# Eight gated blocks on one core: where remainders, preparations and the 32-largest search are placed

## The chip, the core and the metric

The kernel runs on one core of a Trainium2 chip. The metric is the device time of one execution in microseconds (us), lower is better. Engines: PE (TensorE, the matmuls), VectorE (DVE), ScalarE (ACT), GpSimd (POOL), and the queue SP, which issues the DMAs. Each engine executes its own instructions in the order in which the program holds them, and waits on semaphores for the others.

## The reference

Eight sequences of 256 tokens with 128 features pass through four pairs of blocks. Each block reads the layer norm of x and adds its result to x, scaled by a tanh gate:

```
x = x + tanh(g_xattn[0]) * L0_xattn(layernorm(x), ctx)   # causal linear attention, 16 heads
x = x + tanh(g_ffn[0])   * L0_ffn(layernorm(x))          # self attention, 16 heads, plus 8 experts (top 2)
x = x + tanh(g_xattn[1]) * L1_xattn(layernorm(x), ctx)   # 8 heads of 64, only the 64 largest scores of a row
x = x + tanh(g_ffn[1])   * L1_ffn(layernorm(x))          # 8 experts (top 2) and a shared one
x = x + tanh(g_xattn[2]) * L2_xattn(layernorm(x), ctx)   # attention, 16 heads of 8
x = x + tanh(g_ffn[2])   * L2_ffn(layernorm(x))          # 8 wide experts (top 2) and a shared one
x = x + tanh(g_xattn[3]) * L3_xattn(layernorm(x), ctx)   # 16 heads of 8, only the 32 largest scores of a row
x = x + tanh(g_ffn[3])   * L3_ffn(layernorm(x))          # 16 experts in the q, k, v and output projections of one head
```

## The kernel before, in words

The eight sequences form four groups of two (g = 0 to 3); a group is 512 tokens, four tiles of 128. x stays on the chip (xs[g]). For one group a block is a stage, named x0, f0, f1, x2, f2 and f3 in the code (cross attention and feed-forward part of blocks 0 to 3). The attentions of blocks 1 and 3 are no such stages: they choose the 64 or 32 largest scores of a row, a long job for VectorE, and run as one second stream beside all others.

So two streams of Python generators write the program. `others` goes through the stages in a fixed list: x0(0), x0(1), f0(0), x0(2), f0(1), x0(3), f0(2), f1(0), f0(3), x2(0), f1(1), f2(0), x2(1), f1(2), f2(1), x2(2), f1(3), f2(2), x2(3), f2(3), f3(0) to f3(3). Each stage has a share: 40 for x0, 53 for f0, 35 for f1, 75 for x2, 80 for f2, 95 for f3, which makes 1512 in all, and f3(0) begins at 1132. `largest_scores` runs the 64-largest stage (block 1) and then the 32-largest stage (block 3). `side_by_side` always lets that stream emit that stands at the lower position. `T_START` gives the second stream its positions on the same scale: the start of the 64-largest stage, its end, the start of the 32-largest stage, the position at three quarters of it, and its end. A stream that may not go on yet yields None, and the other one goes ahead.

A tile scheduler then orders the recorded instructions; what stands in an engine's queue follows these positions closely, but not to the letter.

Three gates tie the streams together. A group enters the 64-largest stage when its f0 is settled (`started`), f1(g) waits for that stage (`largest_1`). A group enters the 32-largest stage when its f2 is settled (`middle`). f3(0) waits until groups 0 and 2 have left that stage (`largest_3`).

The search stages work in 32 chunks each: eight batches (one sequence each) of four chunks. For the 32-largest stage a chunk is four heads, 8 rows of scores for each partition. The steps of one chunk k:

- `fetch(k)`: scores on PE (line 420), copied to a room in SBUF by ScalarE (427).
- `largest`: four rounds of MAX8 (385) and MATCH_REPLACE8 (389) on VectorE for each of the 8 rows, 32 MAX8 in all; the mask on GpSimd (392). Half way, `fetch(k + 1)` is emitted.
- `weigh(k - 1)`, beside the search of the next chunk: the row's maximum is taken from the scores by `shifted` (for block 3 two transposes on PE, line 1382, and an addition to qT on VectorE, line 1383), then the scores once more on PE (574), the mask added by matmuls (584), the exponential eK on ScalarE (599), and the products with v. After the fourth chunk of a batch, `finish` transposes back, divides (`heads_back`, 341 to 348) and projects out (`out_proj`, 319 to 333), once for each of the two tiles, and adds to x (`add_gated`, 290).

Helpers spread such work. `Ahead(steps, gen)` takes steps of a generator as the neighbouring body goes on: `up_to(f)` at share f of the body. In `others` the end of a stage (its remainder: the last out projections, the addition to x) is taken during the first 30% of the next body, after which the stage counts as settled; the next stage's preparation (layer norm, router, first q, k, v) is taken from 30% to 90%:

```
behind.up_to(f / 0.3)
if f > 0.3:
    settle()
    ...
        ahead.up_to((f - 0.3) / 0.6)
```

In the search stage `weigh` is such a remainder too, with 4 steps, or 12 after the last chunk of a batch.

Other lines named below: the scores of x2 and f0 for their maxima (687, reduced on VectorE at 695) and for the weights (723); f2's matmuls (1476 and 1445, Gelu at 1477); f1's (1269); f3's (1580, 1581 with w3a; 1582, 1635 with w3b; the scaled inputs xe at 851). f2 loads two 256 KB weights an expert, f3 loads w3a and w3b once, all on SP.

Of the kernel before, what the change touches and what calls it, by code (L numbers as in the profile page):

```python
# [14 lines left out]
ALU = mybir.AluOpType  # L15
AX = mybir.AxisListType

P = 128
D = 128
B = 8  # L20
S = 256
# [69 lines left out]
def gated_blocks_kernel(ctx: ExitStack, tc: tile.TileContext, a, out):  # L91
# [9 lines left out]
    def program(exact):  # L101
# [8 lines left out]
        def bank(name="bank"):  # L110
            return psum.tile([P, 512], F32, tag="bank", name=name, bufs=4)
# [8 lines left out]
        def out2(name):  # L120
            return act.tile([P, 512], F32, tag="out2", name=name, bufs=6)
# [165 lines left out]

        def add_gated(g, t, src, gate):

            nc.vector.scalar_tensor_tensor(xs[g][:, t, :], src, gate, xs[g][:, t, :], ALU.mult, ALU.add)  # L290

        def heads_T(w, src, bias, scale, tag):

# [23 lines left out]
            nc.scalar.copy(va[:, :, :, 0:8], pp.rearrange("p t (h d) -> p t h d", d=8))  # L317
            return va

        def out_proj(g, t, o_sb, chunks, w, bias, gate):  # L320

            pt = bank("pt_o")
            for c in range(chunks):
                nc.tensor.transpose(pt[:, c * P : (c + 1) * P], o_sb[:, c * P : (c + 1) * P], ident)
            oT = out2("oT")
            nc.scalar.copy(oT[:, 0 : chunks * P], pt[:, 0 : chunks * P])
            yield
            po = bank("po")
            for c in range(chunks):
                nc.tensor.matmul(  # L330
                    po[:, 0:D], lhsT=oT[:, c * P : (c + 1) * P], rhs=w[:, c, :], start=(c == 0), stop=False
                )
            nc.tensor.matmul(po[:, 0:D], lhsT=bias, rhs=biases, start=False, stop=True)
            add_gated(g, t, po[:, 0:D], gate)

        def heads_back(g, bb, oTs, done):

            for qc in range(2):
                pn = bank("pn").rearrange("p (c r d) -> p c r d", c=4, r=4)
                for c in range(4):  # L340
                    nc.tensor.transpose(
                        pn[:, c].rearrange("p r d -> p (r d)"), oTs[c // 2][:, c % 2, qc * P : (qc + 1) * P], ident
                    )
                rec = small.tile([P, 4, 4], F32, tag="rec", name="rec")
                nc.vector.reciprocal(rec, pn[:, :, :, 8])
                o_sb = out2("o_sb")[:, 0:D].rearrange("p (c r d) -> p c r d", c=4, r=4)
                nc.vector.tensor_tensor(
                    o_sb, pn[:, :, :, 0:8], rec.unsqueeze(3).to_broadcast([P, 4, 4, 8]), ALU.mult
                )
                yield  # L350
                yield from done(g, 2 * bb + qc, o_sb.rearrange("p c r d -> p (c r d)"))

        def chunk_products(o, va, c, es):

# [41 lines left out]
        def attention_largest(  # L396
# [9 lines left out]
            NP = R // 2  # L406
            NJ = 2 * R
            batches = [(g, bb) for g in groups for bb in range(2)]
            ready, ahead, masks, shifts, placed = {}, {}, {}, {}, {}
            n = len(batches) * 4  # L410

            def fetch(k):
# [117 lines left out]
            def keep_largest(k):  # L530
# [25 lines left out]
                for j in range(NJ):  # L556
# [3 lines left out]
                        accum_out=dropped[:, NJ * k + j : NJ * k + j + 1],  # L560
                    )

            def weigh(k):

                i, c = divmod(k, 4)
                qT, kT, va = ready[i]
                mask = masks.pop(k)
                row = shifted(shifts.pop(k), qT, c)
                yield
                sps = [pair("sw").rearrange("p (r n q) -> p r n q", r=2, n=2) for _ in range(NP)]  # L570
                for m in range(2):
                    for r in range(R):
                        rs = slice(rows * r, rows * r + rows)
                        nc.tensor.matmul(  # L574
                            sps[r // 2][:, r % 2, m, :], lhsT=kT[rs, c, m * P : (m + 1) * P], rhs=qT[rs, c, :],
                            start=(m == 0), stop=False,
                        )
                for r in range(R):
                    for m in range(2):
                        sp = sps[r // 2][:, r % 2, m, :]  # L580
                        if row is not None:
                            nc.tensor.matmul(sp, lhsT=pick[:, r : r + 1].to_broadcast([P, P]), rhs=row, start=False, stop=False)
                        for qc in range(2):
                            nc.tensor.matmul(  # L584
                                sp[:, qc * P : (qc + 1) * P], lhsT=mask[:, r, qc, m * P : (m + 1) * P], rhs=drop,
                                start=False, stop=(m == 1 and qc == 1),
                            )
                if dropped is not None and not search:

                    for h in range(NP):  # L590
                        kept = act.tile([P, NJ // NP, S], BF16, tag="s", name="kept", bufs=2)
                        nc.scalar.activation(  # L592
                            kept, mask[:, 2 * h : 2 * h + 2].rearrange("p r q k -> p (r q) k"), AF.Copy,
                            accum_out=dropped[:, NP * k + h : NP * k + h + 1],
                        )
                es = []
                for sp in sps:
                    e = work("eK").rearrange("p (r n q) -> p r n q", r=2, n=2)
                    nc.scalar.activation(e, sp, AF.Exp)  # L599
# [52 lines left out]
            for k in range(steps):  # L652
                for f in units(k):
                    if f is not None:
                        behind.up_to(f)
                        look_ahead(k, f)
                    yield None if f is None else (k + f) / steps
                behind.finish()

                done = k - 1  # L660
                if 0 <= done < n:
                    behind = Ahead(4 if done % 4 < 3 else 12, weigh(done))
            for _ in alongside((x / 12 for x in range(1, 13)), behind):
                yield 1.0

# [412 lines left out]

        class block0_ffn:
            def __init__(self, g):  # L1080
                def done(g, t, o):
                    add_gated(g, t, o, tgf[:, 0:1])
                    yield

                self.g, self.att = g, attention_T(g, self.operands, done)
# [256 lines left out]
        def context_operands(n, weights, k=""):  # L1342
            wq, wk, wv, wo, bq, bk, bo = weights
            norms = {}

            def prepare(g, bb):
                if g not in norms:
                    norms[g] = yield from layer_norm(g)
                xnT = norms[g][1][:, bb * S : (bb + 1) * S]
                cT = ctxT[:, g * W + bb * S : g * W + (bb + 1) * S]  # L1350
                kT = heads_T(wk, cT, bk, 1.0, "kT" + k)
                yield
                qT = heads_T(wq, xnT, bq, INV_SQRT8, "qT" + k)
                yield
                return qT, kT, values16(wv, cT, 32, "va" + k)

            def done(g, t, o):
                yield from out_proj(g, t, o, 1, wo.unsqueeze(1), bo, tgx[:, n : n + 1])
                yield

            return prepare, done
# [353 lines left out]

        T_START = (140, 595, 600, 1140, 1330)

        def stages():  # L1720

# [77 lines left out]
        def others():  # L1799
# [12 lines left out]
            for i, (g, share, may, prep, steps, body, after) in enumerate(todo):  # L1812
                if ahead is None:
                    settle()
                    while not may():
                        yield None
                    ahead = Ahead(steps, prep())
                while ahead.step():
                    yield t
                operands, ahead = ahead.value, None  # L1820
                gen = body(operands)
                following = todo[i + 1] if i + 1 < len(todo) and todo[i + 1][0] != g else None
                while True:
                    try:
                        f = next(gen)
                    except StopIteration as end:
                        settle()
                        behind, done = end.value, after
                        break
                    behind.up_to(f / 0.3)  # L1830
                    if f > 0.3:
                        settle()
                        if following and following[2]():
                            if ahead is None:
                                ahead = Ahead(following[4], following[3]())
                            ahead.up_to((f - 0.3) / 0.6)
                    yield t + share * f
                t += share
            settle()
# [48 lines left out]
```

## Time and profile before

| | before |
|---|---|
| device time, median of 3 runs | 2550.43 us (2545.41 to 2565.9) |
| profiled execution | 2546.42 us, span 2544.7 us |
| mean granted TensorE clock | 0.862 |
| PE busy | 2123.7 us (83%), 12068 records |
| VectorE busy | 1762.5 us (69%) |
| ScalarE busy | 1149.0 us (45%) |
| GpSimd busy | 879.8 us (35%) |
| DMA | 32.97 MB, 13 GB/s over the span |
| the 32-largest stage, first to last MAX8 of line 385 | 1192.5 to 2347.4 us |
| first f3 matmul (line 1580) | 2135 us |

Busy is the share of the span in which an engine has an instruction in work; a PE that is busy need not be at its peak, since matmuls are pipelined and slow down with the granted clock. A fp32 matmul of the program leaves two records. The 40 digits of a slice row stand for 63.6 us each, in tenths.

### The profile page before, as it was taken

How to read it: one execution, taken by the hardware profiler on the slowest of the kernel's cores; microseconds unless marked ns; L12 is line 12 of the kernel's file. 1: busy time of each engine (PE TensorE's matmuls, PEld its weight loads, DVE VectorE, ACT ScalarE, POOL GpSimd, SP SyncE). 2: the span in 40 equal slices, each digit the busy share in tenths (PEclk: the TensorE clock that was granted, in tenths of full speed). 3: DMA queues.
4: the chain of work that ended last, by engine and by line, in shares of the span. 5: the costliest groups of instructions: out<-in, count | busy, mean ns of one | idle time of the engine just before them, and what ended most of it. 6: DMA issues, size and time to landing. Idle time of an engine off the chain costs nothing.

```text
span 2544.7 us, 35734 instructions
## 1 busy us (share of the span) xinstructions
PE 2123.7 (83%) x12068; PEld 1292.4 (51%) x12094; DVE 1762.5 (69%) x5463; ACT 1149.0 (45%) x2437; POOL 879.8 (35%) x2252
## 2 busy tenths in 40 slices
PE   7998888887878778888989868899676975988898
PEld 5655455554445444445444435445343444666677
DVE  4635757756765667665899879894798869798332
ACT  2236556546554677864355433464333542322101
POOL 3104434434432464531334324341233334233000
PEclk8999889978988889998599966899775986999999
DMA  2000001000000000010001100021000110000000
GB/s 63 6 1 2 1 1 32 1 1 1 1 1 1 1 26 1 26 34 22 1 1 42 34 1 1 1 59 50 1 1 1 42 42 1 1 5 1 5 5 6
DMA packets 47896, 32.97 MB, mean 13 GB/s; under 512 B 4747, under 2 KB 42838, under 8 KB 47702
## 3 DMA queue, kind: packets, MB, share of 16 engines
q1 hardware_dynamic: 47702, 30.58, 4.2%
q8 instruction: 97, 1.59, 0.3%
q14 instruction: 97, 0.79, 0.1%
HBM read 29.53 MB, written 1.05 MB: 12 GB/s over the span
## 4 chain that ended last, share of the span: by engine, by line
DVE 39%; PE 36%; ACT 13%; POOL 8%; issue 4%; DMA 0%; DVEq 0%; SPq 0%; ACTq 0%; POOLq 0%
DVE m L385 13%; DVE wk L389 12%; ACT signs L495 4%; PE sm L687 3%; PE sw L723 3%; PE ph L1476 3%; PE pp L299 3%; PE y L1445 2%; DVE nmz L695 2%; PE po L1635 2%; ACT sign L495 2%; PE oT L357 2%; PE o L1216 2%; DVE xe L851 2%; DVE list L542 1%
## 5 line engine op out<-in xcount | busy, mean ns | idle before, releaser
L392 POOL TENSOR_SCALAR mask<-rooms,m 128x256 bf16<-128x256 f32 x192 | 223.3, 1163 | 385.5 <-DVE m L385 353.4
L385 DVE MAX8 m<-wk 128x8 f32<-128x256 f32 x768 | 326.8, 426 | 37.0 <-DVE wk L389 0.9
L723 PE MATMUL sw<-qT,kT 32*128 32x256 f32 x1024 | 172.4, 476 | 68.3 <-ACT eK L599 24.1
L695 DVE TENSOR_REDUCE nmz<-sm 128x4 f32<-128x1024 f32 x128 | 154.9, 1219 | 105.1 <-PE sm L687 96.6
L389 DVE MATCH_REPLACE8 wk<-m,wk 128x256 f32<-128x256 f32 x512 | 208.9, 408 | 0.0
L495 ACT ACTIVATE signs<-room,nt 128x256 bf16<-128x256 f32 x288 | 145.9, 507 | 128.7 <-POOL nt L527 78.5
L687 PE MATMUL sm<-kT,qT 32*128 32x256 f32 x1024 | 152.6, 440 | 40.0 <-DVE nmz L695 28.4
L592 ACT ACTIVATE kept<-mask 128x1024 bf16<-128x1024 bf16 x64 | 67.6, 1057 | 227.3 <-POOL mask L392 227.1
L1476 PE MATMUL ph<-xnT,we 128*128 128x512 f32 x288 | 156.2, 638 | 15.5 <-ACT hT L1477 7.4
L723 PEld LDWEIGHTS sw<-qT,kT 32*128 32x128 f32 x1024 | 101.0, 222 | 128.4 <-DVE nmz L695 32.3
L737 ACT ACTIVATE eT<-sw 128x1024 f32<-128x1024 f32 x128 | 129.6, 1019 | 79.9 <-PE sw L723 73.9
L574 PE MATMUL sw<-qTk,kTk 32*128 32x256 f32 (+1 forms) x768 | 120.8, 456 | 53.6 <-DVE qTk L1383 35.2
L1445 PE MATMUL y<-hT,we 128*128 128x512 f32 x288 | 146.0, 620 | 0.6 <-DVE wb_sb L1457 0.6
L687 PEld LDWEIGHTS sm<-kT,qT 32*128 32x128 f32 x1024 | 92.3, 205 | 101.0 <-DVE nmz L695 42.9
L1477 ACT ACTIVATE hT<-ph,b 128x512 f32<-128x512 f32 x144 | 98.4, 686 | 98.8 <-PE ph L1476 94.4
L599 ACT ACTIVATE eK<-sw 128x1024 f32<-128x1024 f32 x96 | 96.6, 1019 | 89.4 <-PE sw L584 88.5
L420 PE MATMUL sp<-kTk,qTk 32*128 32x256 f32 (+1 forms) x768 | 121.1, 448 | 14.8 <-ACT eT L737 6.5
L357 PE MATMUL oT<-eT,va 128*32 128x256 f32 x1024 | 120.6, 449 | 10.2 <-ACT eT L737 9.3
L392 POOL TENSOR_SCALAR mask<-room,m 128x256 bf16<-128x256 f32 x64 | 74.5, 1164 | 155.2 <-DVE m L385 152.8
L574 PEld LDWEIGHTS sw<-qTk,kTk 32*128 32x128 f32 (+1 forms) x768 | 71.5, 212 | 96.1 <-issue 42.4
L420 PEld LDWEIGHTS sp<-kTk,qTk 32*128 32x128 f32 (+1 forms) x768 | 72.5, 209 | 59.5 <-issue 17.0
L387 POOL TENSOR_SCALAR nmk<-m 128x1 f32<-128x1 f32 x256 | 59.5, 232 | 100.7 <-DVE m L385 100.6
(381 smaller groups left out, 4976.2 us busy)
## 6 DMA issues: line engine op xcount, KB each, us to landing
we<-in_L_ffn_exp_w_dram SPq DMA_DIRECT2D x64, 256.0 KB
we<-in_L_ffn_shared_w_dram SPq DMA_DIRECT2D x8, 256.0 KB
x<-in_x_dram SPq DMA_DIRECT2D x4, 256.0 KB
big_ctx<-in_ctx_dram SPq DMA_DIRECT2D x4, 256.0 KB
w1f<-in_L_ffn_fc_w_dram SPq DMA_DIRECT2D x1, 1024.0 KB
w3a<-in_L_ffn_q_proj_dram SPq DMA_DIRECT2D x4, 256.0 KB
w3a<-in_L_ffn_k_proj_dram SPq DMA_DIRECT2D x4, 256.0 KB
w3b<-in_L_ffn_v_proj_dram SPq DMA_DIRECT2D x4, 256.0 KB
```

What stands on the lines that cost most here:

```text
L357: nc.tensor.matmul(o[32 * r : 32 * r + 32, :], lhsT=va[:, n, 4 * c + r, :], rhs=es[r // 2][:, r % 2, n, :], start=(n == 0), stop=(n == 1),)
L385: nc.vector.max(m8, src[:, j, :])
L389: nc.vector.match_replace(wk[:, j, :], m8, src[:, j, :], LOWEST)
L392: nc.gpsimd.tensor_scalar(mask[:, j, :], s[:, j, :], m8[:, 7:8], 1.0, ALU.is_lt, ALU.mult)
L420: nc.tensor.matmul(sps[r // 2][:, r % 2, qc, :], lhsT=qT[rs, c, qc * P : (qc + 1) * P], rhs=kT[rs, c, :], start=(qc == 0), stop=(qc == 1),)
L495: nc.scalar.activation(to, s[:, j, :], AF.Sign, bias=nt[:, j : j + 1], accum_out=acc[:, j : j + 1])
L574: nc.tensor.matmul(sps[r // 2][:, r % 2, m, :], lhsT=kT[rs, c, m * P : (m + 1) * P], rhs=qT[rs, c, :], start=(m == 0), stop=False,)
L687: nc.tensor.matmul(sps[r // 2][:, r % 2, j, :], lhsT=qT[rs, 2 * cp + j, qc * P : (qc + 1) * P], rhs=kT[rs, 2 * cp + j, :], start=(j == 0), ...
L695: nc.vector.tensor_reduce(nmz[:, qc, 2 * cp : 2 * cp + 2, 2 * h : 2 * h + 2, 8].rearrange("p c r -> p r c"), sps[h], AX.X, ALU.max, negate ...
L723: nc.tensor.matmul(sps[r // 2][:, r % 2, n, :], lhsT=kT[rs, c, n * P : (n + 1) * P], rhs=qT[rs, c, :], start=(n == 0), stop=(n == 1),)
L1445: nc.tensor.matmul(y, lhsT=w2[:, c, :], rhs=hs[c // 2][:, js], start=(c == 0), stop=(c == 3))
L1476: nc.tensor.matmul(pp[:, js], lhsT=w1[:, c * P : (c + 1) * P], rhs=xnT, start=True, stop=True)
```

## The change

The positions of the search stages move: (140, 595, 600, 1140, 1330) becomes (150, 595, 610, 1170, 1380). Remainders of a stage are taken over 40% of the next body in place of 30%, preparations from 40% to 90% in place of 30% to 90%. `weigh` has 3 and 11 steps in place of 4 and 12, and the shift by the maxima is taken out of it: `shift_scores` emits it for chunk k - 1 beyond 0.6 of step k, where `weigh` emitted it at the start of step k + 1. `heads_back` collects both tiles of a batch in one o_sb and calls `done` once, one yield later; `out_proj` and `add_gated` then treat both tiles together. The two projections still take a pair of matmuls each.

```diff
         def add_gated(g, t, src, gate):
 
-            nc.vector.scalar_tensor_tensor(xs[g][:, t, :], src, gate, xs[g][:, t, :], ALU.mult, ALU.add)
+            x = xs[g][:, 2 * t : 2 * t + 2, :] if len(src.shape) == 3 else xs[g][:, t, :]
+            nc.vector.scalar_tensor_tensor(x, src, gate, x, ALU.mult, ALU.add)
...
-        def out_proj(g, t, o_sb, chunks, w, bias, gate):
+        def out_proj(g, bb, o_sb, w, gate, bias):
 
             pt = bank("pt_o")
-            for c in range(chunks):
-                nc.tensor.transpose(pt[:, c * P : (c + 1) * P], o_sb[:, c * P : (c + 1) * P], ident)
-            oT = out2("oT")
-            nc.scalar.copy(oT[:, 0 : chunks * P], pt[:, 0 : chunks * P])
+            for qc in range(2):
+                nc.tensor.transpose(pt[:, qc * P : (qc + 1) * P], o_sb[:, qc * P : (qc + 1) * P], ident)
+            oT = out2("oT")[:, 0:S]
+            nc.scalar.copy(oT, pt[:, 0:S])
             yield
-            po = bank("po")
-            for c in range(chunks):
-                nc.tensor.matmul(
-                    po[:, 0:D], lhsT=oT[:, c * P : (c + 1) * P], rhs=w[:, c, :], start=(c == 0), stop=False
-                )
-            nc.tensor.matmul(po[:, 0:D], lhsT=bias, rhs=biases, start=False, stop=True)
-            add_gated(g, t, po[:, 0:D], gate)
+            po = bank("po")[:, 0:S].rearrange("p (t d) -> p t d", t=2)
+            for qc in range(2):
+                nc.tensor.matmul(po[:, qc, :], lhsT=oT[:, qc * P : (qc + 1) * P], rhs=w, start=True, stop=False)
+                nc.tensor.matmul(po[:, qc, :], lhsT=bias, rhs=biases, start=False, stop=True)
+            add_gated(g, bb, po, gate)
 
         def heads_back(g, bb, oTs, done):
 
+            o_sb = out2("o_sb")[:, 0:S]
             for qc in range(2):
...
-                o_sb = out2("o_sb")[:, 0:D].rearrange("p (c r d) -> p c r d", c=4, r=4)
                 nc.vector.tensor_tensor(
-                    o_sb, pn[:, :, :, 0:8], rec.unsqueeze(3).to_broadcast([P, 4, 4, 8]), ALU.mult
+                    o_sb[:, qc * P : (qc + 1) * P].rearrange("p (c r d) -> p c r d", c=4, r=4), pn[:, :, :, 0:8],
+                    rec.unsqueeze(3).to_broadcast([P, 4, 4, 8]), ALU.mult,
                 )
                 yield
-                yield from done(g, 2 * bb + qc, o_sb.rearrange("p c r d -> p (c r d)"))
+            yield
+            yield from done(g, bb, o_sb)
...
+            def shift_scores(k):
+
+                if 0 <= k < n:
+                    i, c = divmod(k, 4)
+                    rows_of[k] = shifted(shifts[k], ready[i][0], c)
+
             def weigh(k):
...
-                row = shifted(shifts.pop(k), qT, c)
-                yield
+                shifts.pop(k)
+                row = rows_of.pop(k)
...
                     if f is not None:
+                        if f > 0.6 and k - 1 not in rows_of:
+                            shift_scores(k - 1)
                         behind.up_to(f)
                         look_ahead(k, f)
                     yield None if f is None else (k + f) / steps
+                if k - 1 not in rows_of:
+                    shift_scores(k - 1)
                 behind.finish()
 
                 done = k - 1
                 if 0 <= done < n:
-                    behind = Ahead(4 if done % 4 < 3 else 12, weigh(done))
+                    behind = Ahead(3 if done % 4 < 3 else 11, weigh(done))
...
-        T_START = (140, 595, 600, 1140, 1330)
+        T_START = (150, 595, 610, 1170, 1380)
...
-                    behind.up_to(f / 0.3)
-                    if f > 0.3:
+                    behind.up_to(f / 0.4)
+                    if f > 0.4:
                         settle()
...
-                            ahead.up_to((f - 0.3) / 0.6)
+                            ahead.up_to((f - 0.4) / 0.5)
```

The callers follow: block 0's `done` hands both tiles to `add_gated`, block 2's and 3's hand them to `out_proj` in one call.

More of the change, by code (lines that the diff above doesn't have):

```diff
@@ L408, in attention_largest @@
             batches = [(g, bb) for g in groups for bb in range(2)]
-            ready, ahead, masks, shifts, placed = {}, {}, {}, {}, {}
+            ready, ahead, masks, shifts, placed, rows_of = {}, {}, {}, {}, {}, {}
             n = len(batches) * 4
@@ L1080, in __init__, with done @@
             def __init__(self, g):
-                def done(g, t, o):
-                    add_gated(g, t, o, tgf[:, 0:1])
+                def done(g, bb, o):
+                    add_gated(g, bb, o.rearrange("p (t d) -> p t d", t=2), tgf[:, 0:1])
                     yield
@@ L1355, in prepare, with done @@
                 return qT, kT, values16(wv, cT, 32, "va" + k)
-            def done(g, t, o):
-                yield from out_proj(g, t, o, 1, wo.unsqueeze(1), bo, tgx[:, n : n + 1])
+            def done(g, bb, o):
+                yield from out_proj(g, bb, o, wo, tgx[:, n : n + 1], bo)
                 yield
```

## The prediction

> **What bounds the kernel now.** I read the page first (busy shares by slice and the chain that ended last), then the times of line 385's MAX8 instructions (32 to a chunk of the 32-largest stage), then the windows between these times, then PE's waits.
>
> ```profile
> PE   7998888887878778888989868899676975988898
> DVE  4635757756765667665899879894798869798332
> PEclk8999889978988889998599966899775986999999
> DVE m L385 13%; DVE wk L389 12%; ACT signs L495 4%; PE sm L687 3%; PE sw L723 3%; PE ph L1476 3%; PE pp L299 3%; PE y L1445 2%; DVE nmz L695 2%; PE po L1635 2%; ACT sign L495 2%; PE oT L357 2%; PE o L1216 2%; DVE xe L851 2%; DVE list L542 1%
> ```
>
> Two engines take turns. PE is at 8 to 9 tenths nearly everywhere except in a few slices from the 24th on, where VectorE stands at 9; a quarter of the chain is the 32-largest search (lines 385 and 389). The windows cut the program at the search's own marks: before it, chunks 0-7, 8-15, 16-23, 24-31, and the rest after its last MAX8.
>
> ```profile
> 190.00:1192.00 1002.00, 837.92 (x5126) 490.34 (x5135) 651.57 (x1916) 602.85 (x1537) 424.43 (x1518) 0.88 0.03 10
> 1192.50:1482.30 289.80, 255.69 (x1223) 132.13 (x1227) 246.80 (x813) 137.60 (x207) 105.07 (x157) 0.85 0.06 17
> 1482.30:1797.50 315.20, 271.11 (x1350) 144.96 (x1350) 249.86 (x811) 141.63 (x213) 107.55 (x158) 0.82 0.08 23
> 1797.50:2071.10 273.60, 201.20 (x966) 106.26 (x964) 222.27 (x769) 109.48 (x180) 105.19 (x152) 0.74 0.07 20
> 2071.10:2347.40 276.30, 218.43 (x1312) 165.62 (x1313) 241.97 (x798) 72.33 (x131) 93.05 (x149) 0.86 0.01 2
> 2347.40:2544.70 197.30, 170.16 (x897) 139.97 (x894) 60.34 (x105) 24.73 (x63) 4.86 (x11) 0.93 0.02 5
> ```
>
> Columns: length, busy us of PE, its weight loads, VectorE, ScalarE and GpSimd, granted clock, DMA. Neither engine is full in any of them, although each is full in parts. Two parts show why:
>
> ```profile
> 1908.00:1963.00 55.00, 33.14 (x149) 18.09 (x149) 51.25 (x180) 15.43 (x25) 23.43 (x36) 0.53 0.00 1
> 1736.00:1797.00 61.00, 58.60 (x336) 32.50 (x335) 23.54 (x34) 27.58 (x44) 4.83 (x4) 1.00 0.12 36
> 2098.10:2127.90 29.80, 8.94 (x35) 6.36 (x31) 28.59 (x125) 7.25 (x19) 14.06 (x21) 0.50 0.00 1
> ```
>
> In the first and third the search runs nearly alone: VectorE 93 to 96% busy, PE 60 and 30%. In the second the search has run out of allowed chunks (group 2 may start only when f2 of that group has settled) and PE alone works, VectorE at 39%. A chunk running alone takes 27 us; chunk 7 took 65.9, chunk 15 100.5, chunk 23 61.2. This alternation is what the change can move.
>
> **The change, part by part.** Durations are means of the trace; the order of the instructions is that of the two built programs. PE's total work differs by 7 us and VectorE's by -7 in 2124 and 1763: the change moves work, it removes hardly any.
>
> *The search drawn out (T_START).* Positions are units of the neighbours' shares. Before, three quarters of the search's 34 steps lie on 600 to 1140 (21.2 units a step), after on 610 to 1170 (22.0); the last quarter on 190 units, then on 210. I weighted each PE instruction with the mean time of its line (986 ns for an L1476 matmul, 925 for L1445, 283 for L687, 315 for L723, 448 for L1580, 526 for L1635) and summed the neighbours' PE work between two fetches (L420) of the search. The last stretch of each group, in which VectorE starves, shrinks: chunk 7 from 83.4 to 64.3 us of neighbours' PE work, chunk 15 from 108.3 to 87.2, chunk 23 from 48.5 to 24.2; the steps ahead of them gain as much (108.6 to 130.3, 88.8 to 111.6, 69.6 to 92.5). The work behind the last fetch falls from 208.3 to 181.0. Group by group:
>
> - Chunks 0-7. Saved at the end 19.1 / 0.93 (PE's share in chunk 7) = 20.5 us. PE was busy 194 of the 224 us ahead of it, 11 us of the idle time in chunk 0, which gets nothing. So 19 us can absorb 21.7. All absorbed: -20; none: 0. PE is near its limit (255.7 of 289.8), so I take -6.
> - Chunks 8-15. Saved 21.1 / 0.95 = 22; idle PE time ahead 39 us, 22 of it in chunks 8 and 9, which get nothing. Between -22 and 0, -10 (it also keeps the two waits below).
> - Chunks 16-23. Saved 24.3 / 0.86 = 28. Ahead of it PE is idle 64 of 212 us and VectorE sets the pace, so the added 22.9 us is mostly hidden: steps of 24 to 33 us of PE against 27 of VectorE. If that cover is gone, it costs 23. Between -28 and 0, -18.
> - Chunks 24-31. In the new order block 3's first expert batch (f3, group 0) stands ahead of the fetch for chunk 26, where it stood behind it: 42.3 us of PE work against 0.5. It fills chunk 25's idle PE (the 0.50-clock row above), but the fetch waits behind it: VectorE has 24.1 + 16.8 us there against 51.7 on PE, so a stall of about 11 us, where chunk 26 had 18. Against that, these chunks now carry 152 us of neighbours' PE work instead of 124, and 52 of VectorE's instead of 45. VectorE needs 8 x 24.1 + 52 = 245 of the 276 us. Between -10 and +25; I take +6.
> - After the last chunk: 27.3 us less PE work, at 0.86 busy (170.16 of 197.30) 32 us; part of it runs beside chunk 31 anyway. Between -32 and -15, -26.
>
> *Maxima a step sooner, two tiles together.* Both take a wait from PE:
>
> ```profile
> PE sw L574 <- DVE qTk L1383: 35.2, 8, 10.6
> PE pt_o L324 <- DVE o_sb L347: 33.0, 13, 8.2
> ```
>
> The transposes of the shifts (L1382) and the addition on VectorE (L1383, 410 ns) move from the start of a step to 0.6 of the step before, ahead of the score matmuls; the out projection now starts one yield after the second tile's o_sb. Queued behind such a wait are the neighbour's matmuls and the next fetch. But 26.6 + 12.0 + 5.9 of the 68 us lie where VectorE sets the pace or in the mixture of chunks 24-31; only 21 lie in chunks 8-15, where PE is fuller. They are in the sums above, not added again. What is late next is L1383, which waits for PE's transposes: 10.1 us in 6 before; it can double. The 16 saved copies (L326, 265 ns each against about 372 for a 128x256 copy) and 24 fewer additions (344 ns, a 128x256 one about 472) are a few us on engines with room.
>
> *ScalarE's tables.* The new order has ten more table loads: 6 ahead of eK (L599), 2 for Gelu, 2 for Silu.
>
> ```profile
> L599 ACT ACT_TABLE_LOAD x22 | 28.2, 1283 | 3.2 <-PE sw L584 2.8
> L326 ACT COPY oT<-pt_o 128x128 f32<-128x128 f32 x32 | 8.5, 264 | 39.9 <-PE pt_o L324 39.9
> ```
>
> That is 12.8 us on an engine 45% busy, but an exponential stands between two PE steps: between 0 and 13, I take +4. The Trainium skill ("ScalarE: Activation LUTs", What ACT_TABLE_LOAD costs) adds a drain of about 1380 ns to each switch, which would make it 27 us in place of 12.8. The trace does not show the drain: at 1966.13 the load follows a read-out that ended within 0.1 us, and the next activation starts 0.02 us after it.
>
> *Remainders over 40%, preparations over 40 to 90%.* Same instructions, other places; f2 of a group settles 0.1 of a body later (619 to 627 units for group 0, 809 to 817, 999 to 1007). That is in the positions above. *DMA.* SP has the same 285 rows. The eight 256 KB loads of w3b were issued at 2040 and moved within 12 us, while their first reader ran at 2136; starting half a chunk sooner leaves that covered.
>
> *Before 1192 us.* The neighbours' PE work between two fetches of the 64-largest stage moves both ways, 914 to 916 in all: 0, between -15 and +15.
>
> Sum: -6 - 10 - 18 + 6 - 26 + 4 = -50 on the profiled run's 2546.4 us (span 2544.7): 2496. The median of the three runs is 2550.4, 4 us above; I forecast 2498.
>
> **The rivals.**
> 1. *Nothing left (within 1%).* PE is the real limit of chunks 0-15 (88 and 86% with pipelining counted as busy), so moved work costs what it saves; chunks 24-31 go to +25 and eat the end. -18 - 26 + 25 + 4 = -15: 2535. For it: chunks 1, 3, 4 and 5 show PE at 93 to 95%. Against: chunks 16-22 with PE 54 to 77%.
> 2. *Slower by the clock.* The granted clock follows how closely PE is fed: 1.00 in the burst, 0.53 beside the search. An L1476 matmul takes 592 ns in bursts and up to 1221 in the slow parts. The change takes 19 + 21 + 24 + 27 us out of bursts into the search's steps. If these stay near 0.55, the moved 91 us cost twice (182), and the neighbours' work already there (108.6 + 88.8 + 69.6 = 267 us) stretches by 0.3 (+80) as the mean clock falls from 0.81 to 0.62. Saved at the ends: 20 + 22 + 28 + 32 = 102. PE's idle time in these steps hides 19 + 17 + 64 = 100. 182 + 80 - 102 - 100 = +60: 2606. It decides if the mean clock of the search's first 24 chunks falls under 0.70. Against: 1960-2003 with PE 92% busy had 0.82.
>  The Trainium skill ("TensorE: Matmul & The Clock Gate", Part 1) states that activity over about 3.4 us releases a half-rate clock. By that rule fuller steps should raise it, which speaks for rival 3; the trace's 0.53 at 60% busy and 1.00 at 96% agree.
> 3. *More than forecast.* The clock rises in the filled steps and both waits vanish. With PE at 0.95 in chunks 0-15 (-20 and -30), VectorE at 0.93 in 16-23 (-35) and 0.92 PE from 2071 on (-52) the floor is 2409; half of that beyond my sum gives 2450.
>
> **How the numbers follow.** Forecast 0.52 (own range 2465 to 2525), nothing left 0.20, slower 0.15, more 0.13. About 1% is what a measurement of this kernel can tell from no change (its runs lie 0.8% apart): faster is under 2525, slower above 2576. Faster 0.52 + 0.13 = 0.65, same 0.20, slower 0.15. For 8 in 10 the range reaches from 2450, leaving half of the third rival out, to 2562, above rival 1 and leaving out the clock.
>
> **What would show it.** Right: chunks 7, 15 and 23 at about 47, 80 and 36 us; chunk 25 with f3's matmuls and PE above 60%; the windows beside the search at a clock of 0.7 or more in chunks 19-22; the end after the last MAX8 near 170 us; the waits of L574 on L1383 and of L324 on L347 under 15 us each. Wrong: chunks 4, 6, 10 or 13 longer by all that the group's end saves; a mean clock under 0.70; chunk 25 or 26 stalled over 30 us; the search starting later than 1205 us.

## The result and the profile after

The changed kernel takes 2531.43 us (median of 14 runs, 2510.27 to 2539.7) where the kernel before takes 2548.98 on the same chip: a ratio of 0.9913, 95% interval 0.989 to 0.9937. That is 0.9% faster. I had forecast 2498 from 2550.43, 52 us less; it is 17.6 us less, so the direction was right and the size about three times too large. The first rival, "nothing left", had named 2535.

The page's slices and its chain, which answer to those of before:

```profile
PE   7999889888798877889799886899876966977898
DVE  4634856866765767753999959986598885899432
PEclk9989988888898889997699866999676978998999
DVE m L386 13%; DVE wk L390 12%; ACT signs L496 6%; PE sm L698 3%; PE sw L734 3%; PE pp L300 2%; ACT sign L496 2%; PE y L1456 2%; PE ph L1487 2%; PE po L1646 2%; DVE nmz L706 2%; PE oT L358 2%; PE pqk L1591 2%; PE pqk L1592 2%; PE pv L1593 2%
```

The same chain, the same two lines of the search at its head. The windows, cut at the same marks (search not begun, chunks 0-7, 8-15, 16-23, 24-31, rest; columns as before):

```profile
190.00:1193.80 1003.80, 864.22 (x5184) 501.13 (x5194) 651.88 (x1907) 605.33 (x1541) 426.01 (x1520) 0.88 0.03 9
1193.80:1482.70 288.90, 253.43 (x1222) 133.05 (x1224) 246.53 (x813) 137.49 (x204) 105.27 (x157) 0.83 0.06 17
1482.70:1796.70 314.00, 265.06 (x1344) 141.47 (x1351) 248.68 (x808) 141.61 (x210) 106.95 (x157) 0.83 0.08 23
1796.70:2046.90 250.20, 187.19 (x942) 100.16 (x944) 217.35 (x764) 117.22 (x182) 104.55 (x151) 0.80 0.06 17
2046.90:2353.40 306.50, 238.12 (x1381) 181.27 (x1382) 252.38 (x807) 73.74 (x134) 93.37 (x151) 0.86 0.02 6
2353.40:2519.60 166.20, 147.40 (x827) 122.54 (x825) 49.87 (x93) 22.70 (x56) 4.76 (x10) 0.98 0.02 5
```

Against before: the search starts 1.3 us later, chunks 0-7 take 0.9 us less, 8-15 1.2 less, 16-23 23.4 less, 24-31 30.3 more, the end 31.1 less. The profiled span is 25 us shorter, and nearly all of it is chunks 16-23. What the end saves, chunks 24-31 pay.

In chunks 24-31 one step stands out. From the timeline of the changed kernel, start and length in us, PE and then VectorE:

```profile
2099.42 0.62 PE L838 MATMUL pt_r<-ident_b,r_w 128*48 128x128 bf16 x4 [14.70 <-POOL r_w L370]
2103.81 1.22 PE L1591 MATMUL pqk<-xe,w3a 128*128 128x256 f32 x2 [1.23 <-DVE xe L862]
...
2141.95 1.13 PE L421 MATMUL sp<-kTk,qTk 32*128 32x256 f32 x8
```

```profile
2106.24 0.43 DVE L386 MAX8 m<-wk 128x8 f32<-128x256 f32 x1
...
2144.24 0.43 DVE L386 MAX8 m<-room 128x8 f32<-128x256 f32 x1 [2.69 <-ACT room L428]
```

VectorE ends the search of chunk 25 at 2106.7 and starts that of chunk 26 at 2144.2. It waits for a room that ScalarE fills (line 428) from the first half of the fetch for chunk 26 (line 421, 2141.95), and this fetch stands in PE's queue behind a whole f3 batch. Chunk 25 takes 70.4 us in place of 29.9, chunk 26 then 37.8 in place of 52.8: together 25.5 of the 30.3 us by which chunks 24-31 grow.

The two waits of PE, after:

```profile
PE sw L581 <- DVE qTk L1394: 4.5, 2, 2.7
PE pt_o L325 <- DVE o_sb L346: 20.0, 7, 8.7
```

Of 35.2 us the first keeps 4.5, of 33.0 the second 20.0.

### The profile page after: what moved, and what is told of

It reads as the page before. It is cut to its first block, busy times and chain, and to the rows that moved or that the text cites. A ratio compares the mean times of both kernels' runs of the same rounds, so it can differ in the third digit from the quotient of the medians.

```text
span 2519.6 us, 35700 instructions
## 1 busy us (share of the span) xinstructions
PE 2126.2 (84%) x12066; PEld 1293.4 (51%) x12094; DVE 1757.8 (70%) x5439; ACT 1156.5 (46%) x2431; POOL 880.5 (35%) x2252
## 4 chain that ended last, share of the span: by engine, by line
DVE 37%; PE 36%; ACT 14%; POOL 8%; issue 5%; DMA 0%; DVEq 0%; SPq 0%; ACTq 0%; POOLq 0%
DVE m L386 13%; DVE wk L390 12%; ACT signs L496 6%; PE sm L698 3%; PE sw L734 3%; PE pp L300 2%; ACT sign L496 2%; PE y L1456 2%; PE ph L1487 2%; PE po L1646 2%; DVE nmz L706 2%; PE oT L358 2%; PE pqk L1591 2%; PE pqk L1592 2%; PE pv L1593 2%
## 5 line engine op out<-in xcount | busy, mean ns | idle before, releaser
L698 PE MATMUL sm<-kT,qT 32*128 32x256 f32 x1024 | 164.2, 462 | 24.2 <-DVE nmz L706 15.6
L698 PEld LDWEIGHTS sm<-kT,qT 32*128 32x128 f32 x1024 | 98.0, 214 | 89.0 <-DVE nmz L706 35.2
L421 PE MATMUL sp<-kTk,qTk 32*128 32x256 f32 (+1 forms) x768 | 117.4, 445 | 10.6 <-DVE nmz L706 3.8
L386 DVE MAX8 m<-rooms 128x8 f32<-128x256 f32 x192 | 78.6, 410 | 25.1 <-ACT rooms L428 25.1
```

What stands on the lines that cost most here:

```text
L386: nc.vector.max(m8, src[:, j, :])
L421: nc.tensor.matmul(sps[r // 2][:, r % 2, qc, :], lhsT=qT[rs, c, qc * P : (qc + 1) * P], rhs=kT[rs, c, :], start=(qc == 0), stop=(qc == 1),)
L698: nc.tensor.matmul(sps[r // 2][:, r % 2, j, :], lhsT=qT[rs, 2 * cp + j, qc * P : (qc + 1) * P], rhs=kT[rs, 2 * cp + j, :], start=(j == 0), ...
```

## The experiments

Each is set against the kernel before by its ratio, and by its own profile, cut at the search's MAX8. All lengths in us; "start" is the first MAX8 of the 32-largest stage, "0-7" the length of chunks 0 to 7, "f3 part" chunks 24-31 plus the end, c7 chunk 7. A ratio is taken against runs of the kernel before on the same chip.

```
kernel         ratio (95% interval)     start  0-7    8-15   16-23  24-31+end = f3 part   c7    c15    c23   c25   c26
before         1                        1192.5 289.8  315.2  273.6  276.2+197.3 = 473.5   65.9  100.5  61.2  29.9  52.8
before_again   (one profile)            1195.9 289.5  316.9  274.0  278.9+200.1 = 479.0   65.5  102.1  61.7  29.9  53.4
after          0.9913 (0.989-0.9937)    1193.8 288.9  314.0  250.2  306.5+166.2 = 472.7   67.9  100.0  40.7  70.4  37.8
after_again    (one profile)            1186.0 289.8  302.1  251.2  309.9+166.2 = 476.1   66.3   87.6  40.7  74.0  37.8
a_t0           1.0045 (1.0009-1.008)    1224.5 285.6  311.9  263.8  280.5+198.0 = 478.5   71.0  104.9  63.0  45.7  32.9
b_t            0.997 (0.9954-0.9986)    1219.8 283.2  307.8  264.3  315.9+165.8 = 481.7   63.4   94.8  43.6  29.9  79.3
b_joint        0.9984 (0.9969-0.9999)   1227.6 285.3  311.2  267.4  274.1+193.6 = 467.7   65.1   97.8  63.5  48.9  31.0
a_shift0       0.9936 (0.9915-0.9958)   1204.4 296.6  306.5  255.3  307.5+168.6 = 476.1   73.0   90.9  42.3  71.4  38.8
a_rem0         0.9913 (0.9878-0.9948)   1215.4 290.1  307.2  257.2  306.2+172.6 = 478.8   72.9   90.1  42.5  72.1  38.1
a_jump         0.9863 (0.9821-0.9905)   1195.0 289.7  304.6  253.1  300.5+171.4 = 471.9   66.3   89.2  42.3  40.2  44.3
a_settle       1.0024 (1.0004-1.0044)   1178.5 298.9  308.2  288.3  311.9+166.3 = 478.2   57.1   68.4  41.4  74.8  37.7
a_early        0.9762 (0.9726-0.9798)   1192.8 289.3  302.3  253.2  274.4+180.2 = 454.6   68.5   87.6  42.4  36.9  31.4
a_both         0.9922 (0.9892-0.9952)   1191.1 304.0  308.2  288.8  280.5+167.0 = 447.5   57.1   68.4  41.9  36.8  31.4
b_early        0.9944 (0.9912-0.9976)   1196.0 287.2  314.4  273.6  267.5+196.2 = 463.7   63.3  100.5  61.2  43.7  33.3
a_less         (one profile)            1185.7 287.2  303.7  253.8  306.9+168.8 = 475.7   66.2   89.3  41.8  74.4  37.8
a_r3           (one profile)            1193.8 289.8  302.1  251.3  268.5+183.4 = 451.9          c24 19.1, c25 71.5
a_r3_first     (one profile)            1195.0 280.2  293.8  253.1  309.7+172.7 = 482.4   95.6   99.7  42.4  75.0  38.2
```

**Both kernels once more: how far one kernel differs from itself.** No edit.

> The kernel before, profiled once more, to see how far one kernel's stages differ from execution to execution. Theory 1 (the parts up to 1192 us and chunks 0-15 vary by 10 to 30 us with the clock, the later cuts do not): the search starts between 1192 and 1228 us; chunks 16-23 within 5 us of 273.6, chunk 23 at 61, the end at 197. Theory 2 (the stages repeat within 3 us, so that differences between kernels there are the kernels'): start at 1192.

> The changed kernel, profiled once more. Theory 1: the search starts anywhere from 1192 to 1228 us; chunk 25 again near 70 us, chunks 24-31 plus the end within 5 us of 472.7. Theory 2: every stage within 3 us of the first profile.

The cuts repeat within 4 us, except the start (1186 and 1194 in the changed kernel), the f3 part by 5.5 in the kernel before, and chunk 15 of the changed kernel, 100.0 and 87.6 us. So the 23 us of chunks 16-23 and the two opposite 30 us behind them are the kernels' own. The start lies 6.5 us ahead of the kernel before in the second profile, earlier than either theory of after_again had it.

**The positions alone, taken out and put in.**

```diff
 a_t0, on the changed kernel
-        T_START = (150, 595, 610, 1170, 1380)
+        T_START = (140, 595, 600, 1140, 1330)
 b_t, on the kernel before: the reverse
```

> The changed kernel with the positions of before (140, 595, 600, 1140, 1330). Theory 1 (the positions alone bring the gain of chunks 16-23 and of the end, the rest of the change nothing or a small loss by the fetch of chunk 26 behind 24 us of f3): chunks 16-23 back at about 274 us, the part after the last MAX8 at about 197, chunk 25 at about 48: 2545-2560 us. Theory 2 (the waits removed from PE by the joint outputs and the earlier maxima carry the gain): 2525-2535 us still.

> The kernel before with the new positions alone. Theory 1: chunks 16-23 near 250 us, the end near 163; the f3 burst stands ahead of the fetch of chunk 27 (69 us in place of 44), so chunk 26 stalls longer, 70 us in place of 53: 2525-2540 us, as the whole change. Theory 2: without the other parts the time stays at 2545-2555.

Theory 1 holds for the places: chunk 23 is 61 to 64 us with the old positions and 41 to 44 with the new, and the end 194 to 200 and 166 to 173 us, but for a_early and a_r3, which change the f3 part itself. b_t's chunk 26 stalls for longer than said (79.3). It does not hold for the sum: alone the positions bring 0.3%, and without them the rest costs 0.45%. In both profiles the search starts at 1220 to 1225, some 30 us later than in before and after; b_joint and, in part, a_rem0 show the same. That is lost in the 64-largest stage, and why stays open. One sign: up to the start the mean granted clock is 0.86 to 0.88 in these four kernels and 0.88 to 0.89 in before and after (two profiles each); no run tests it. The 30 us are as large as what is to be explained, so the two runs don't tell how the gain divides between the positions and the rest.

**Both tiles together, alone.** On the kernel before, `add_gated`, `out_proj`, `heads_back` and the two callers as in the change, all else as before.

> The kernel before with both tiles' outputs together, alone. Theory 1 (a remainder of fewer steps settles before the fetch of chunk 26, which then stands behind 24 us of f3): PE's wait for o_sb falls from 33 to under 15 us, chunk 25 grows to 45-50 and chunk 26 falls to about 38, the time within 5 us of before: 2545-2555. Theory 2 (the wait of 33 us was on the path): 2515-2530.

Theory 1 in the time: 0.16% faster. The wait for o_sb is 23.5 us, not under 15. Chunk 25 grows to 48.9 and chunk 26 falls to 31.0: the remainder settles before the fetch of chunk 26, as the order said, and one stall takes the place of another.

**The maxima at the start of the step again.**

```diff
-                        if f > 0.6 and k - 1 not in rows_of:
-                            shift_scores(k - 1)
...
-                if k - 1 not in rows_of:
-                    shift_scores(k - 1)
                 behind.finish()
 
                 done = k - 1
                 if 0 <= done < n:
+                    shift_scores(done)
```

> The changed kernel with the shift by the maxima emitted at the start of the next step again. Theory 1 (PE's wait for the addition lies beside the search or is taken up by the next gate): that wait is back near 30 us, the time 2525-2540 us, within 0.4% of the change. Theory 2 (the wait is on the path): 15 to 30 us longer than the change, 2545-2560.

The wait is back at 18.6 us, the ratio 0.9936 against 0.9913, with intervals that overlap. No loss of 15 to 30 us shows, so theory 1 stands: the wait was off the path for the most part. An effect of up to some 0.4% can't be told from none.

**Remainders over 30% again.** `f / 0.3`, `f > 0.3`, `(f - 0.3) / 0.6` in `others`.

> The changed kernel with remainders over 30% and preparations over 30 to 90% again. Theory G (chunks 7 and 15 last as long as the gate: the next group may start only when the remainder of f2 is settled at 40% of x2's body, and x2's attention runs meanwhile): they shorten by 5 to 12 us each; 2510-2525 us. Theory P (PE's total work sets chunks 0-15): both within 3 us, 2528-2535.

A ratio of 0.9913, that of the change itself. Chunk 7 did not shorten (72.9), and chunk 15 (90.1) lies near the lower of the changed kernel's own two values. Theory G is not borne out; this part of the change is worth nothing that can be measured.

**f3's first batch shared out over the fetches.**

```diff
                     while not may():
                         yield None
+                    if i == 20:
+                        t += 45
...
-        T_START = (150, 595, 610, 1170, 1380)
+        T_START = (150, 595, 610, 1170, 1425)
```

> The changed kernel with the neighbours' position raised by 45 units when f3(0) begins, and 1425 in place of 1380, so that f3's first batch is shared out over the fetches of chunks 26 to 28: 13, 29 and 28 us of f3's matmuls ahead of them in place of 42, 32 and 13. Theory 1 (the search starves in chunk 25 because its next fetch stands behind a whole f3 batch, 37 us): chunk 25 falls from 70 us to under 45, chunks 24-31 from 306 to 270-285, the time to 2495-2512 us. Theory 2 (chunks 24-31 are long because more f3 work lies in them, wherever it stands): they stay at 295 or more, the time at 2525-2535.

The stall goes (chunk 25 40.2 us), and the f3 part stays: 471.9 against 472.7 to 476.1. The other chunks take up what the stall gave. Theory 1 falls in its main claim: the stall is real, but it is not the price. The interval of the ratio, 0.9821 to 0.9905, overlaps with the change's.

**Less search in chunks 24-31.** Three rounds of MAX8 for k >= 24.

> The changed kernel with three rounds of MAX8 in place of four in chunks 24 to 31 (the 24 largest of group 3 in place of 32): 8 x 8 x 0.86 = 55 us less VectorE work there. Theory 1 (from f3's first batch on, f3's own chain on PE with the search's PE work added is the limit): only chunks 24 and 25, where the search runs alone, are shorter, by 7 us each; chunks 24-31 plus the end fall from 473 to 455-462. Theory 2 (VectorE sets the pace up to the last MAX8): the sum falls by 40 to 55, to 418-433.

With 55 us less VectorE work the f3 part falls by 21 to 24 us, of which 8 are chunk 24. That is a little beyond theory 1 (11 to 18) and far from theory 2 (40 to 55). VectorE alone does not pace this part, though over a third of what it lost comes through. Theory 1's places were not right either: chunk 25 did not shorten (71.5), chunks 26-31 did by 31 us, and the end grew by 17.

**f3 allowed earlier.** f3(0) waited for group 2's last projection. It needs group 0's result and the rooms in which w3b lands, and these are free once chunk 23 is searched. (`freed` is an empty set made beside `largest_3`.)

```diff
             for k in range(steps):
+                if not search and k == 24:
+                    freed.add(k)
...
-                    if g not in largest_3 or (g == 0 and NG - 2 not in largest_3):
+                    if g not in largest_3 or (g == 0 and (24 not in freed if not exact else NG - 2 not in largest_3)):
```

> The changed kernel with f3(0) allowed from the step of chunk 24 on (the rooms that w3b takes are free then), in place of after group 2's last projection. Theory C (from chunk 24 on the sum is f3's own chain plus the two steps in which the search runs alone): chunk 25 under 45 us, chunks 24-31 plus the end from 473 to 440-455; 2500-2515 us. Theory D (VectorE sets it): within 8 us of 473.

> The kernel before with f3(0) allowed from the step of chunk 24 on, all else as before. Theory C (from chunk 24 on the sum is f3's chain plus the steps in which the search runs alone): chunks 24-31 plus the end fall from 474-479 to 448-460 us, the time to 2525-2538. Theory D (the gain of a_early needs the new positions, the old ones put f3's batches so that VectorE is the limit): less than 8 us.

a_early takes 2495.92 us, 0.9762 of the kernel before, and beats both kernels. Chunk 25 falls from 70.4 to 36.9 us, chunk 24 grows from 27.0 to 44.4, since f3 now begins beside it. Its last two windows:

```profile
2037.60:2312.00 274.40, 221.44 (x1312) 167.99 (x1312) 244.12 (x801) 72.53 (x131) 93.23 (x150) 0.88 0.01 4
2312.00:2492.10 180.10, 160.14 (x882) 133.26 (x882) 56.26 (x100) 23.46 (x58) 4.74 (x10) 0.96 0.02 6
```

PE is busy 381.6 us in 454.5, where it was busy 385.5 in 472.7: the saving is for the most part idle PE time, 73 us in place of 87. The f3 part is 18 to 21 us shorter. Between the ratios 0.9913 and 0.9762 there are 38 us; what the rest is stays open, but chunk 15 takes 87.6 us here as in the second profile of the changed kernel, against 100.0 in the first. On the kernel before the same edit brings 0.56% and an f3 part shorter by 10 to 15 us, less than expected (463.7 against 448 to 460) and more than theory D's 8; f3 still leaves more for the end there (196.2). An earlier start of f3 pays in both kernels, as theory C says, in the kernel before at about two thirds of the size that it has in the changed one.

**A stage settled as soon as its remainder is taken.**

```diff
-                    if f > 0.4:
+                    if f > 0.4 or behind.taken >= behind.steps:
                         settle()
+                    if f > 0.4:
                         if following and following[2]():
```

> The changed kernel, but a stage counts as settled as soon as all steps of its remainder are taken (for f2 one step, at the start of the next body), in place of 40% into it. Theory G: the stalls at the ends of the first two groups go, chunk 7 from 67 to under 50, chunk 15 from 88-100 to under 75, chunks 0-15 from 592-603 to 540-570; chunks 16-23 may give back up to 10; 2475-2510 us. Theory P: the same work lies elsewhere, chunks 0-15 together stay within 10 us, 2520-2535.

> a_settle and a_early together. Theories G and C: 2445-2490 us, chunks 0-15 at 540-570 and chunks 24-31 plus the end at 440-455. If either is wrong, only the other's share: 2475-2515.

The stalls do shrink: chunk 7 to 57.1, chunk 15 to 68.4. The sum does not: chunks 0-7 grow by 9 to 10, 8-15 stay, 16-23 grow by 37 to 38, and the whole is 0.24% slower than before, slower than either theory allowed. x2's attention, which ran behind the gate while VectorE waited, now runs between the search's steps and stretches these: its last score matmuls for the maxima (line 698) run from 1758 to 1780 us in the changed kernel, inside chunk 15, and from 1811 to 1849 in a_settle, in chunk 17, which takes 44.5 us in place of 28.0. a_both has an f3 part 7 us below a_early's and pays the same 37 us in chunks 16-23; it too lies beyond what was expected (0.9922).

**Less of either stream in chunks 0-15.** a_less drops two of nine experts in f2 of groups 0 and 1. a_r3_first takes three rounds for k < 16.

> The changed kernel with f2 of groups 0 and 1 leaving out two of its nine experts (so the result lacks them): 2 x 4 x (986 + 925) ns = 15.3 us less PE work in chunks 0-7 and as much in chunks 8-15, hardly any VectorE work. Theory 1 (chunks 0-15 are set by the neighbours' PE stream, so that moving it saves nothing and removing it does): chunks 0-7 fall from 289 to 272-277, chunks 8-15 from 314 to 297-302, the rest stays. Theory 2 (VectorE and waits set them): both within 5 us.

> The changed kernel with three rounds in place of four in chunks 0 to 15 (the 24 largest for groups 0 and 1): 8 x 0.86 = 6.9 us less VectorE work a chunk, 55 a group. Theory V (VectorE's order with its waits sets chunks 0-6 and 8-14, and x2's attention behind the gate chunks 7 and 15): chunks 0-7 fall from 289 to 235-250, chunks 8-15 from 302-314 to 250-270. Theory S (the neighbours' stream sets the group's length, the search only fills it): chunks 0-6 shorten, but chunk 7 and 15 grow by as much, and both sums fall by less than 15.

I had misplaced one f2 in the first: f2(0) runs before the search starts and f2(1) beside chunks 3 to 7, so only chunks 0-7 lost 15 us of PE work, and the statement on chunks 8-15 tests nothing. Chunks 0-7 of the changed kernel (second profile), of a_less, and of a_r3_first, the last cut at 1380.0, where chunk 7 begins (1379.7):

```profile
1186.00:1475.80 289.80, 254.46 (x1226) 133.59 (x1224) 246.63 (x813) 137.20 (x204) 105.37 (x157) 0.84 0.06 17
```

```profile
1185.70:1472.90 287.20, 245.66 (x1192) 130.78 (x1190) 245.85 (x810) 132.69 (x196) 102.53 (x155) 0.80 0.05 14
```

```profile
1195.00:1380.00 185.00, 161.17 (x796) 83.60 (x798) 150.38 (x528) 100.69 (x148) 88.61 (x135) 0.89 0.05 15
1380.00:1475.20 95.20, 85.65 (x427) 46.44 (x426) 41.99 (x93) 37.08 (x56) 16.61 (x22) 0.80 0.08 23
```

Fifteen us less PE work bring 2.6 us: PE's busy time falls by 9 only, at a clock of 0.80 in place of 0.84. By its own words that is theory 2, but the clock changed with the work: 113 us of these chunks ran at half clock in place of 96, which is worth about 8 us (an estimate, half of the 17). So this run doesn't settle whether PE's work sets chunks 0-7. Fifty-five us less VectorE work bring 9 us: chunks 0-6 shorten to 185 from 221, and chunk 7 grows from 68 to 96, with VectorE busy for 42 us of it and PE for 86. Chunks 8-15 fall to 293.8 from 302.1 and 314.0, with chunk 15 at 99.7. That is theory S: VectorE's sum does not set these groups. That the neighbours' stream up to the gate sets them fits all these runs; no run shows it alone.

## Why the prediction was wrong in size

- *Chunks 16-23, -18.* Right: -23.4 (-22 in the second profile). The neighbours' PE work moved into steps that VectorE paced, and chunk 23 fell from 61.2 to 40.7. The clock of these chunks rose from 0.74 to 0.80 in the first profile; in the second it was about 0.76, at the same length.
- *Chunks 24-31, +6, and the end, -26.* Here the prediction failed. The measured +30.3 and -31.1 cancel. The forecast span was 50 us shorter and the profiled one is 25; this +30.3 in place of +6 is 24 of the 25 us that are missing (the other differences lie between -5 and +9 and cancel). The step that was wrong is "VectorE needs 8 x 24.1 + 52 = 245 of the 276 us", from which I took it that 28 us more of f3 would find room beside the search. The f3 part holds at 468 to 482 us under five other arrangements (a_t0, b_t, b_joint, a_jump and the change), with the stall in chunk 25, in chunk 26 or spread. It moved by more only where f3 could start sooner (a_early 455, a_both 448, b_early 464) or search was taken out (a_r3 452). So where in it the search lies does not count. My reading is that its length is f3's own sequence of dependent steps, with what the search's work adds and the steps in which the search runs alone. No run takes f3's own work out, so that part is argued and not shown, and PE's own work (busy 385.5 of 472.7 us) is a rival to it.
- *The stall "of about 11 us".* It was 37.6, beyond the 30 us that I had named as a sign of being wrong. I set chunk 25's VectorE work against f3's PE work as if they ran together, but f3's matmuls start at 2103.8, 3 us before the last MAX8: PE first waits 14.7 us for the router's weights, whose VectorE steps stand between the MAX8s. As a_jump shows, this error did not cost the 37 us: there chunk 25 is 30 us shorter and the f3 part the same.
- *Chunks 0-7, -6, and 8-15, -10.* Measured -0.9 and -1.2 in the first profile, 0.0 and -13.1 in the second. Work did leave the ends of the groups (chunk 7 has 309 PE records in place of 336), but chunk 7, for which I had named 47 us, did not shorten. Its windows in the kernel before and in the changed one, then a part of the latter:

```profile
1416.40:1482.30 65.90, 61.50 (x336) 34.25 (x329) 45.53 (x114) 30.50 (x50) 16.88 (x21) 0.92 0.10 31
1414.80:1482.70 67.90, 62.88 (x309) 35.11 (x307) 39.20 (x109) 28.58 (x47) 15.29 (x21) 0.77 0.05 16
1447.90:1478.70 30.80, 30.80 (x120) 17.88 (x118) 8.26 (x8) 8.24 (x13) 0.00 (x0) 0.50 0.00 1
```

PE is busy in all of the last 30.8 us, with x2's matmuls, at half the clock. The records of the granted clock hold two values in every run, 0.5 and 1.0. So a mean of 0.92 over 65.9 us is 10 us at half clock, and 0.77 over 67.9 us is 31; the second profile has 31 too. If such a stretch costs half its length, the 21 us more cost about 10 us (an estimate), which takes back a saving of that size. Chunk 15 did shorten: in the four profiles in which its clock was 0.98 to 1.00 (after_again, a_jump, a_early, a_r3, all with the change's order up to there) chunks 8-15 are 10.6 to 13.1 us shorter than before, as forecast. In the first profile its clock was 0.86, and the gain was gone. No run changes the clock alone. For the rest, a_settle and a_r3_first show that what leaves chunk 7 comes back in chunks 0-6, and the other way round.

- *The two waits, "under 15 each".* 4.5 for the maxima, 20.0 for o_sb. Taking the first to be mostly off the path was right (a_shift0); that the second would go was not.
- *ScalarE's tables, +4.* Ten more loads are there (72 against 62, 28 of them ahead of eK). No run isolates them. What stands just ahead of the load at 1966.13 is an activation (line 797, ended at 1966.11) and not the read-out; the gap is as small as I said.
- *Before 1192 us, 0 between -15 and +15.* Right for the whole change (+1.3 and -6.5). Single parts of it start the search up to 35 us later, beyond my bounds; that stays open. By its own terms the sum is 2496 for the profiled run and 2500 for the median; the 2498 lies between.
- *The rivals.* "Slower by the clock" needed a mean under 0.70 in the first 24 chunks; they had 0.83, 0.83 and 0.80. The filled steps did get more clock (chunks 8-14 0.82 in place of 0.75). It was a burst that lost it (chunk 7 0.77 in place of 0.92), where neither I nor this rival had looked; and "the granted clock follows how closely PE is fed" does not hold there, with PE busy throughout at 0.50. "More than forecast" had no room, since the f3 part did not give. "Nothing left" was the case, and for half of its reason: chunks 24-31 came to +30 and ate the end. Its 0.20 was too low: the profile showed two rows, 276 and 197 us, that touch, and I let the saving of one stand with a small charge on the other.
- *The signs.* Of those named for being right, chunk 23 (40.7 us), the end (166.2), PE above 60% in chunk 25 (63%) and the wait for the maxima (4.5) came; chunk 7 (67.9), chunk 15 in the first profile (100.0) and the wait for o_sb (20.0) did not. Of those for being wrong, the stall of over 30 us in chunk 25 came.

## What to carry to other kernels

When two streams are interleaved, a change of positions pays only in a stretch where one engine waits for an agreed order and nothing else; add up both sides of each cut, because what one side saves the other can give back. Before sharing work out, ask what holds the next stage's first instruction: here a gate that waited for longer than it had to cost 18 to 21 us in the changed kernel, about as much as the whole change brought (17.6 us). Take work out of each stream in turn to see whether a sum of one engine's busy time means anything there, and read the granted clock of the same stretch before the result: in a_less it had changed with the work.

## What was not expected of the hardware

The same program took 100.0 us for chunk 15 in one execution and 87.6 in another, with the same instructions in the same order. The windows of that chunk in the two profiles of the changed kernel, first and second:

```profile
1696.70:1796.70 100.00, 93.18 (x456) 48.77 (x458) 52.17 (x122) 40.94 (x63) 18.24 (x23) 0.86 0.09 27
```

```profile
1691.50:1779.10 87.60, 81.42 (x468) 42.78 (x467) 52.17 (x121) 41.78 (x63) 17.42 (x24) 1.00 0.10 31
```

(The second window lies 1.2 us behind the chunk's own marks, 1690.3 and 1777.9; between these the length and the clock are the same.) VectorE has 52.17 us of work in both; the granted clock is 0.86 in one and 1.00 in the other, and x2's score matmuls (line 698) reach 791 ns in the first and 479 in the second, at a median of 374 in both. The difference lies in one piece, near the end of the chunk, where x2's matmuls run. First and second profile:

```profile
1765.40:1792.70 27.30, 27.30 (x104) 15.40 (x100) 6.18 (x6) 6.87 (x11) 0.00 (x0) 0.50 0.00 1
```

```profile
1751.00:1778.00 27.00, 24.93 (x202) 14.81 (x194) 11.69 (x14) 11.20 (x19) 0.10 (x1) 1.00 0.00 1
```

In the first PE is busy without a pause for 27.3 us and the clock stays at 0.50; in the second about twice as many matmuls pass in the same time. Half of 27.3 us is about the 12.4 us by which the chunks differ. What starts or ends such a piece, no run here shows. The 12.4 us stand against 17.6 for the whole change. The 14 runs of the changed kernel spread over 29 us (2510.27 to 2539.7), and the shorter ones have the higher mean clock: 0.871 at 2510.27, 0.867 at 2521.4 to 2524.04, and 0.861 to 0.864 from 2528.34 on.
